# Attention scores of a recommender: 25 groups summed in one PSUM bank by wide products instead of one-column products

## The chip, the cores and the metric

The kernel runs on one core of a Trainium2 chip. Its engines are TensorE (PE, with its weight loads shown as PEld), VectorE (DVE), ScalarE (ACT), GpSimd (POOL) and SyncE (SP); each works through its own list of instructions, and semaphores order them against each other. The metric is the device time of one execution in microseconds, as the median of several runs.

## The reference

There are 50,001 items. For each item two small attentions over its 32 neighbours give two 32-vectors (`a_sus`, `a_inf`). Together with a 64-vector from an embedding table they make a row of 128 numbers per item, for an item in a user's history (`h`) and for a target item (`t`). Then, for 16,384 users with 100 history items each:

```
x      = h * t[:, None, :]                       # 16384 x 100 x 128
z      = relu(einsum("bld,hd->blh", x, W1) + b1) # 128 hidden
scores = einsum("blh,h->bl", z, W2[0])           # one number per user and item
exp_A  = exp(scores) * ((history != target[:, None]) & (history != 0))
attn   = exp_A / (sum(exp_A, -1) ** 0.5)[:, None]
s      = sum(h * attn[..., None])                # one number over all users
pred   = sigmoid(cosine(s * ones, t))            # 16384 results
```

Only the sum of each row of `h` is needed behind the attention, so the kernel keeps that sum in column 0 of its table of rows. Everything is float32.

## The kernel before

The first stage builds the table: POOL gathers 64 neighbour vectors per two tiles of 128 items (`v`, lines 131 to 145), DVE and ACT do the small attentions, and the rows go to two tables in the chip's main memory, `table` (129 numbers: the row's sum and the row) and `ttab` (the target's 128).

The second stage, the user stage, is where the change lies. Users come 128 at a time (`c`, 128 blocks); a block's 100 history items are worked off in 25 groups of `LG` = 4 (`g`). A step `s` is one group of one block, so there are 3,200 steps. In one step

- `gather` (lines 295 to 310): POOL issues four indirect DMAs (L302), each fetching one row of 129 numbers for each of 128 users, into a buffer `h`. There are `HBUF` = 20 such buffers, so POOL may be up to 20 steps ahead;
- `turn` (L318): TensorE transposes the four 128x128 pieces into one PSUM bank `hT_ps` (three such buffers, pool `ps_t`);
- `times_target` (L323, L326): DVE multiplies them by the block's transposed targets `tT` into `xT`, and copies the rows' sums into `hsum`. That copy is the last reader of `h`;
- `hidden` (L335, L337): TensorE multiplies `xT` by `w1T` into `z_ps` (128 hidden x 512 columns), ACT adds the bias and takes the Relu into `z`;
- `scored` (L344): for each of the group's four items TensorE loads `z` of 128 users as the weight and multiplies it by the one column `w2_sb`, which gives one column of the block's `score` tile (128 users x 100 items, one PSUM bank, two buffers in pool `ps_s`).

Once per block `target_rows` (L266) gathers the targets, `target_work` (L278 to L293) transposes them by way of an `hT_ps` buffer and builds the mask `keep`; `weights` (L350) takes the exponential of `score` on ACT into `ea`; `ended` (L355 to L358) multiplies by mask and sums and reduces on DVE.

The order on the engines in this stage is that of the program: a loop over `s` issues the pieces with a skew, `hidden` for step `s - LAG` and `scored` for step `s - 2*LAG` (`LAG` = 3), with `weights` and `ended` hung behind a block's last step:

```python
gather(s); turn(s); times_target(s)
if 0 <= s - LAG < last:      hidden(s - LAG)
if 0 <= s - 2 * LAG < last:  scored(s - 2 * LAG)
done, left = divmod(s - 2 * LAG - NG, NG)
if 0 <= done < UC and left == 0: weights(done)
if 0 <= done < UC and left == 2: ended(done)
```

A short last part (L390 on) combines the sums of all blocks into the results.

Of the kernel before, what the change touches and what calls it, by code (L numbers as in the profile page):

```python
# [10 lines left out]
F32 = mybir.dt.float32  # L11
# [3 lines left out]
AF = mybir.ActivationFunctionType  # L15
# [3 lines left out]
P = 128  # L19
# [5 lines left out]
HID = 128  # L25
B = 16384
L = 100
# [14 lines left out]
UC = B // P  # L42
BSUB = 4
LG = 4
NG = L // LG
W = 1 + D
LAG = 3
# [6 lines left out]
def kernel(  # L54
# [13 lines left out]
    nc = tc.nc  # L68
# [4 lines left out]
    const = ctx.enter_context(tc.tile_pool(name="const", bufs=1))  # L73
# [7 lines left out]
    ident = const.tile([P, P], F32, name="ident")  # L81
# [5 lines left out]
    w2_sb = const.tile([HID, 1], F32, name="w2_sb")  # L87
    nc.sync.dma_start(w2_sb, w2.rearrange("o h -> h o"))
    w1_sb = const.tile([HID, D], F32, name="w1_sb")
    nc.sync.dma_start(w1_sb, w1)  # L90
    w1T = const.tile([D, HID], F32, name="w1T")
    with tc.tile_pool(name="wps", bufs=1, space=bass.MemoryType.PSUM) as wps:
        w1_ps = wps.tile([D, HID], F32, name="w1_ps")
        nc.tensor.transpose(w1_ps, w1_sb, ident)
        nc.vector.tensor_copy(w1T, w1_ps)
# [149 lines left out]
    with (  # L245
# [11 lines left out]
        users, hists = {}, {}  # L257
        rows, got, hT, xT, z = {}, {}, {}, {}, {}

        def history_of(i):  # L260
            hists[i] = u_in.tile([P, BSUB, L], I32, name="hidx")
            nc.sync.dma_start(hists[i], hist_v[i])

        def target_rows(c):
            t = u_t.tile([P, D], F32, name="t")
            nc.gpsimd.indirect_dma_start(  # L266
                out=t,
                out_offset=None,
                in_=ttab[0:ITEMS, :],
                in_offset=bass.IndirectOffsetOnAxis(ap=tidx[:, c : c + 1], axis=0),  # L270
            )
            users[c] = {"t": t, "hidx": hists[c // BSUB][:, c % BSUB, :]}

        def target_work(c):
            u = users[c]
            t = u["t"]
            tT_ps = ps_t.tile([P, LG, P], F32, name="hT_ps")
            nc.tensor.transpose(tT_ps[:, 0, :], t, ident)  # L278
            tT = u_t.tile([D, 1, P], F32, name="tT")
            nc.vector.tensor_copy(tT[:, 0, :], tT_ps[:, 0, :])  # L280
            u["tT"] = tT
            nc.vector.tensor_reduce(tsum[:, c : c + 1], t, AX.X, ALU.add)
            junk = u_t.tile([P, D], F32, name="junk")
            nc.scalar.activation(junk, t, AF.Square, accum_out=tsq[:, c : c + 1])
            keep = u_s.tile([P, L], F32, name="keep")
            idf = u_s.tile([P, L], F32, name="idf")
            nc.vector.tensor_copy(idf, u["hidx"])
            nc.vector.tensor_scalar(keep, idf, 0.0, None, ALU.not_equal)
            nc.vector.scalar_tensor_tensor(
                keep, idf, tidf[:, c : c + 1], keep, ALU.not_equal, ALU.mult  # L290
            )
            u["keep"] = keep
            u["hsum"] = u_s.tile([P, L], F32, name="hsum")  # L293
# [17 lines left out]

        def turn(s):
            c, g = divmod(s, NG)
            if g == 0:
                users[c]["score"] = ps_s.tile([P, L], F32, name="score")
            hT[s] = ps_t.tile([P, LG, P], F32, name="hT_ps")
            for q in range(LG):
                nc.tensor.transpose(hT[s][:, q, :], rows[s][:, q, 1:W], ident)  # L318
# [19 lines left out]

        def scored(s):
            c, g = divmod(s, NG)  # L340
            of = z.pop(s)
            for q in range(LG):
                l = g * LG + q
                nc.tensor.matmul(  # L344
                    users[c]["score"][:, l : l + 1], of[:, q, :], w2_sb, start=True, stop=True
                )

        def weights(c):
            users[c]["ea"] = u_s.tile([P, L], F32, name="ea")
            nc.scalar.activation(users[c]["ea"], users[c]["score"], AF.Exp)  # L350

        def ended(c):
            u = users.pop(c)
# [6 lines left out]
        last = UC * NG  # L360
# [1 line left out]
        history_of(1)  # L362
        target_rows(0)
        target_work(0)
        for s in range(last + 2 * LAG + 4):
            c, g = divmod(s, NG)
            if s < last:
                if g == 0 and c % BSUB == 2 and 0 < c // BSUB and c // BSUB + 1 < UC // BSUB:
                    history_of(c // BSUB + 1)
                if g == 5 and c + 1 < UC:  # L370
                    target_rows(c + 1)
                gather(s)
                turn(s)
                times_target(s)
            if 0 <= s - LAG < last:
                hidden(s - LAG)
            if 0 <= s - 2 * LAG < last:
                scored(s - 2 * LAG)
            if s < last and g == 15 and c + 1 < UC:
                target_work(c + 1)  # L380
            done, left = divmod(s - 2 * LAG - NG, NG)
            if 0 <= done < UC and left == 0:
                weights(done)
            if 0 <= done < UC and left == 2:
                ended(done)

    with (
# [12 lines left out]
        s = f_s.tile([P, 1], F32, name="s")  # L400
# [72 lines left out]
```

## Time and profile before

| | |
|---|---|
| median of 3 runs | 36,520.64 us (36,513.01 to 36,525.43) |
| span of the profiled execution | 36,753.4 us |
| first stage, up to POOL's first gather of the user stage | about 17,531 us |
| user stage | about 19,214 us, 6.0 us a step |
| POOL busy | 25,638.7 us (70%) |
| TensorE busy, matmuls and weight loads | 10,978.4 us (30%) and 8,197.0 us (22%) |
| DVE, ACT busy | 6,839.7 us (19%), 2,598.4 us (7%) |
| granted TensorE clock, whole span and user stage | 0.805 and 0.63 |

The page gives the span of the profiled execution as its only time; it is 232.8 us, or 0.6%, longer than the median of the runs. In the views, "x" is a count of instructions, the number in square brackets is the engine's idle time just before an instruction and what ended it, and "issue" means that the profile shows nothing for which the engine waited. A TensorE instruction's row shows when it was started; the ends of matmuls are modelled.

### The profile page before, as it was taken

The page shows a single profiled execution, that of the slowest core. Times are in us where ns is not written, and L with a number is a line of the kernel's source. Part 1 is how long each engine was busy: PE and PEld are TensorE (multiplying, and loading weights), DVE is VectorE, ACT ScalarE, POOL GpSimd, SP SyncE. Part 2 cuts the span into 40 slices and gives each one's busy share as a digit, 9 for nine tenths or more (in the row PEclk, how much of TensorE's full clock was granted, in tenths as well). Part 3 has the DMA queues.
Part 4 walks back from the last instruction along what each step waited for, and adds up shares of the span by engine and source line. Part 5 has one row for each costly group of instructions (what it writes and reads, how often), then busy time and mean ns, then how long its engine had stood idle before and what let it go on. Part 6 is the DMA issues. An engine that isn't in the chain of part 4 may idle for free. (4 is left out here: it accounts for less than half of the span.)

```text
span 36753.4 us, 140646 instructions
## 1 busy us (share of the span) xinstructions
PE 10978.4 (30%) x44931; PEld 8197.0 (22%) x44931; DVE 6839.7 (19%) x9939; ACT 2598.4 (7%) x5572; POOL 25638.7 (70%) x25446
## 2 busy tenths in 40 slices
PE   0000000000000000000455555555555555555555
PEld 0000000000000000000344444444444444444444
DVE  2222222222222222222111111111111111111111
ACT  0000000000000000000011111111111111111111
POOL 7777777777777777777666666666666666666665
PEclk9999999999999999999766666666666666666666
DMA  1111111111111111111222222222222222222221
GB/s 42 29 27 27 28 27 29 27 27 28 27 29 27 27 28 28 28 27 25 46 45 45 46 45 45 45 46 45 45 45 45 45 46 45 46 45 45 45 45 42
DMA packets 1028095, 1364.65 MB, mean 37 GB/s; under 512 B 559904, under 2 KB 614432, under 8 KB 1027360
## 3 DMA queue, kind: packets, MB, share of 16 engines
q0 software_dynamic: 814080, 1265.42, 16.4%
q10 hardware_dynamic: 151056, 51.51, 0.8%
q1 hardware_dynamic: 62224, 38.72, 0.4%
q8 instruction: 363, 5.95, 0.1%
q14 instruction: 372, 3.05, 0.0%
HBM read 1315.31 MB, written 51.50 MB: 37 GB/s over the span
## 5 line engine op out<-in xcount | busy, mean ns | idle before, releaser
L302 POOL DMA_INDIRECT h<-table,hidx x12800 | 12076.4, 943 | 6922.7 <-issue 3842.1
L140 POOL DMA_INDIRECT v<-in_egeo_dram,nidx x12512 | 13440.9, 1074 | 4062.1 <-issue 3999.8
L344 PEld LDWEIGHTS score<-w_sb,z 128*128 128x128 f32 x25600 | 5127.8, 265 | 7371.6 <-issue 7368.3
L344 PE MATMUL score<-w_sb,z 128*128 128x1 f32 x25600 | 4337.7, 273 | 5275.9 <-issue 5198.2
L278 PE MATMUL hT_ps<-ident,t 128*128 128x128 f32 x128 | 48.6, 380 | 17557.8 <-DMA t<-ttab,tidx 17527.4
L335 PE MATMUL z_ps<-xT,w1T 128*128 128x512 f32 x6400 | 5002.9, 868 | 585.1 <-issue 581.7
L323 DVE TENSOR_TENSOR xT<-hT_ps,tT 128x512 f32<-128x512 f32 x3200 | 2189.8, 688 | 15948.5 <-PE hT_ps L318 7577.8
L278 PEld LDWEIGHTS hT_ps<-ident,t 128*128 128x128 f32 x128 | 35.8, 280 | 17561.6 <-issue 17561.6
L318 PE MATMUL hT_ps<-ident,h 128*128 128x128 f32 x12800 | 3056.8, 360 | 2340.2 <-issue 1889.1
L337 ACT ACTIVATE z<-z_ps,b_sb 128x512 f32<-128x512 f32 x3200 | 2137.4, 686 | 17016.2 <-remote 6414.2
L155 DVE TENSOR_TENSOR prod<-v,own_ps 128x4096 f32<-128x4096 f32 x196 | 864.4, 4410 | 12931.3 <-DMA v<-in_egeo_dram,nidx 12931.3
L318 PEld LDWEIGHTS hT_ps<-ident,h 128*128 128x128 f32 x12800 | 2231.2, 206 | 2730.8 <-issue 2200.1
L335 PEld LDWEIGHTS z_ps<-xT,w1T 128*128 128x128 f32 x6400 | 1440.8, 271 | 876.2 <-issue 875.7
L188 DVE TENSOR_TENSOR wv<-v,ex 128x1024 f32<-128x1024 f32 x782 | 1377.4, 1874 | 315.8 <-ACT ex L172 303.1
L172 ACT ACTIVATE ex<-sc,top 128x32 f32<-128x32 f32 x782 | 227.7, 291 | 16999.8 <-DVE sc L162 10385.7
L162 DVE TENSOR_REDUCE sc<-prod 128x128 f32<-128x4096 f32 x196 | 864.5, 4411 | 6.7
L196 DVE TENSOR_REDUCE att<-wv 128x128 f32<-128x4096 f32 x196 | 864.1, 4409 | 6.0
L326 DVE COPY hsum<-h 128x4 f32<-128x4 f32 x3200 | 537.9, 168 | 0.0
L266 POOL DMA_INDIRECT t<-ttab,tidx x128 | 120.7, 943 | 66.2 <-issue 65.3
L280 DVE COPY tT<-hT_ps 128x128 f32<-128x128 f32 x128 | 37.0, 289 | 593.7 <-remote 343.9
L172 ACT ACTIVATION_READ_ACCUMULATOR ex<-sc,top 128x1 f32 x782 | 146.1, 187 | 0.0
L153 ACT COPY own_ps<-own 128x64 f32<-128x64 f32 x391 | 82.2, 210 | 56.9 <-issue 49.3
(50 smaller groups left out, 638.7 us busy)
## 6 DMA issues: line engine op xcount, KB each, us to landing
h<-table,hidx POOLq DMA_INDIRECT x12800
v<-in_egeo_dram,nidx POOLq DMA_INDIRECT x12512
table<-row ACTq DMA_DIRECT2D x22, 1096.5 KB
own<-in_egeo_dram SPq DMA_DIRECT2D x23, 544.0 KB
row<-in_ehist_dram SPq DMA_DIRECT2D x23, 544.0 KB
ttab<-in_etgt_dram ACTq DMA_DIRECT2D x1, 12500.0 KB
ttab<-row ACTq DMA_DIRECT2D x22, 544.0 KB
hidx<-in_history_dram SPq DMA_DIRECT2D x32, 200.0 KB
```

The lines of the kernel that those rows point to most:

```text
L140: nc.gpsimd.indirect_dma_start(out=v[:, m, k].rearrange("p t d -> p (t d)"), out_offset=None, in_=egeo, in_offset=bass.IndirectOffsetOnAxi ...
L155: nc.vector.tensor_tensor(prod[:, 0:n].rearrange("p m k t d -> p m k (t d)"), v.rearrange("p m k t d -> p m k (t d)"), own_ps[:, 0:n].to_b ...
L162: nc.vector.tensor_reduce(sc[:, 0:n].rearrange("p m t k -> p m k t"), prod[:, 0:n], AX.X, ALU.add)
L188: nc.vector.tensor_tensor(wv[:, m, t].rearrange("p d k -> p k d"), subs[b]["v"][:, m, :, t, :], ex[:, m, t, :].rearrange("p (k o) -> p k o ...
L196: nc.vector.tensor_reduce(att[:, 0:n], wv[:, 0:n], AX.X, ALU.add)
L302: nc.gpsimd.indirect_dma_start(out=rows[s][:, q, :], out_offset=None, in_=table, in_offset=bass.IndirectOffsetOnAxis(ap=users[c]["hidx"][: ...
L318: nc.tensor.transpose(hT[s][:, q, :], rows[s][:, q, 1:W], ident)
L323: nc.vector.tensor_tensor(xT[s], hT.pop(s), users[c]["tT"].to_broadcast([D, LG, P]), ALU.mult)
L326: copy = nc.vector.tensor_copy(users[c]["hsum"][:, g * LG : (g + 1) * LG], rows.pop(s)[:, :, 0:1].rearrange("p q o -> p (q o)"),)
L335: nc.tensor.matmul(z_ps, w1T, xT.pop(s), start=True, stop=True)
L337: nc.scalar.activation(z[s], z_ps, AF.Relu, bias=b1_sb)
L344: nc.tensor.matmul(users[c]["score"][:, l : l + 1], of[:, q, :], w2_sb, start=True, stop=True)
```

## The change

A constant tile `pick` is built at the start: 25 small matrices of 128 x 25, all zeros but for `w2` in column `g` of the `g`-th. For each step `scored` now makes one product, with `pick[:, g, :]` as the weight and the step's whole `z` (512 columns) as the moving operand, into a bank of 25 partitions x 512 columns. The products of a block's 25 steps are accumulated in that bank: step `g` adds the scores of its 4 x 128 items and users to partition `g` and zero to all others. `weights` becomes a copy of the bank to SBUF on ACT. A new piece `exponents`, one step later, turns it back with four TensorE transposes (25x128 to 128x25) into a buffer of `ps_t`, and takes the exponential on ACT into `ea`, in the order that `ea` had before. `ended` moves from two steps behind `weights` to four, and the loop runs two steps longer.

```diff
+    pick = const.tile([HID, NG, NG], F32, name="pick")
+    nc.vector.memset(pick, 0.0)
+    for g in range(NG):
+        nc.vector.tensor_copy(pick[:, g, g : g + 1], w2_sb)
...
         def turn(s):
             c, g = divmod(s, NG)
-            if g == 0:
-                users[c]["score"] = ps_s.tile([P, L], F32, name="score")
             hT[s] = ps_t.tile([P, LG, P], F32, name="hT_ps")
...
         def scored(s):
             c, g = divmod(s, NG)
-            of = z.pop(s)
+            if g == 0:
+                users[c]["bank"] = ps_s.tile([NG, LG, P], F32, name="bank")
+            nc.tensor.matmul(
+                users[c]["bank"], pick[:, g, :], z.pop(s), start=g == 0, stop=g == NG - 1
+            )
+
+        def weights(c):
+            flat = u_t.tile([NG, LG, P], F32, name="flat")
+            nc.scalar.copy(flat, users[c].pop("bank"))
+            users[c]["flat"] = flat
+
+        def exponents(c):
+            flat = users[c].pop("flat")
+            score = ps_t.tile([P, LG, P], F32, name="hT_ps")
             for q in range(LG):
-                l = g * LG + q
-                nc.tensor.matmul(
-                    users[c]["score"][:, l : l + 1], of[:, q, :], w2_sb, start=True, stop=True
-                )
-
-        def weights(c):
+                nc.tensor.transpose(score[:, q, 0:NG], flat[:, q, :], ident[0:NG, 0:NG])
             users[c]["ea"] = u_s.tile([P, L], F32, name="ea")
-            nc.scalar.activation(users[c]["ea"], users[c]["score"], AF.Exp)
+            nc.scalar.activation(
+                users[c]["ea"].rearrange("p (g q) -> p q g", q=LG), score[:, :, 0:NG], AF.Exp
+            )
...
-        for s in range(last + 2 * LAG + 4):
+        for s in range(last + 2 * LAG + 6):
...
             if 0 <= done < UC and left == 0:
                 weights(done)
-            if 0 <= done < UC and left == 2:
+            if 0 <= done < UC and left == 1:
+                exponents(done)
+            if 0 <= done < UC and left == 4:
                 ended(done)
```

## The prediction

> **What bounds the kernel now.** I read the page's totals and costliest groups first, then stretches of the user stage, then single instructions in order of time, then the waits and the end of the chain.
>
> ```profile
> PE 10978.4 (30%) x44931; PEld 8197.0 (22%) x44931; DVE 6839.7 (19%) x9939; ACT 2598.4 (7%) x5572; POOL 25638.7 (70%) x25446
> L302 POOL DMA_INDIRECT h<-table,hidx x12800 | 12076.4, 943 | 6922.7 <-issue 3842.1
> L344 PEld LDWEIGHTS score<-w_sb,z 128*128 128x128 f32 x25600 | 5127.8, 265 | 7371.6 <-issue 7368.3
> L344 PE MATMUL score<-w_sb,z 128*128 128x1 f32 x25600 | 4337.7, 273 | 5275.9 <-issue 5198.2
> L335 PE MATMUL z_ps<-xT,w1T 128*128 128x512 f32 x6400 | 5002.9, 868 | 585.1 <-issue 581.7
> L318 PE MATMUL hT_ps<-ident,h 128*128 128x128 f32 x12800 | 3056.8, 360 | 2340.2 <-issue 1889.1
> L337 ACT ACTIVATE z<-z_ps,b_sb 128x512 f32<-128x512 f32 x3200 | 2137.4, 686 | 17016.2 <-remote 6414.2
> ```
>
> No engine is full. Per group of 128x4 rows (3200 groups) TensorE runs 4 transposes, 2 products of 512 columns (float32 takes two passes) and 8 score products of one column, each with its own weight load: 28 instructions, 16 of them for the scores. Now the stretches (columns: the window's length, then busy time and count of PE, PEld, DVE, ACT, POOL, then the clock, the DMA share, GB/s):
>
> ```profile
> 17531.00:36745.00 19214.00, 10977.44 (x44928) 8196.31 (x44928) 2649.56 (x7553) 2192.09 (x3588) 12197.16 (x12928) 0.63 0.20 45
> 17531.00:17570.00 39.00, 15.43 (x30) 5.84 (x31) 5.21 (x15) 1.78 (x4) 26.41 (x28) 1.00 0.27 67
> 24953.90:24961.00 7.10, 7.10 (x43) 5.52 (x42) 2.16 (x6) 2.06 (x3) 5.57 (x6) 0.88 0.22 50
> 24989.40:25002.20 12.80, 12.80 (x63) 9.78 (x64) 3.09 (x8) 2.53 (x5) 9.70 (x11) 0.72 0.21 48
> 25024.30:25038.20 13.90, 13.90 (x50) 10.80 (x51) 3.88 (x12) 3.11 (x5) 10.55 (x12) 0.50 0.21 48
> 24966.90:24987.20 20.30, 3.92 (x14) 3.01 (x13) 0.77 (x2) 0.69 (x1) 12.69 (x14) 0.56 0.21 47
> 25003.70:25022.00 18.30, 4.16 (x10) 2.25 (x10) 0.00 (x0) 0.00 (x0) 11.74 (x13) 0.59 0.22 49
> 24953.90:24989.40 35.50, 18.34 (x94) 13.82 (x93) 4.39 (x13) 4.17 (x7) 22.64 (x24) 0.69 0.20 45
> ```
>
> POOL's gathers, in order of time:
>
> ```profile
> 24953.91 0.94 POOL L302 DMA_INDIRECT h<-table,hidx  x1 [6.02 <-PE hT_ps L318]
> ...
> 24982.61 0.94 POOL L302 DMA_INDIRECT h<-table,hidx  x1 [0.30 <-issue]
> 24989.45 0.94 POOL L302 DMA_INDIRECT h<-table,hidx  x1 [5.89 <-PE z_ps L335]
> ```
>
> First and last are 24 issues: 28.70/23 = 1.248 us each, 4.99 us a group. 12928 issues would take 16,134 us of the stage's 19,214; the other 3,080 us are POOL standing still for a free `h` buffer. That is the most this change can bring. One cycle is 24 issues (6 groups, 30 us) and a stall of 5.6 us beyond the usual gap: 5.93 us a group.
>
> Why buffers are late (DVE's and TensorE's instructions, in order of time):
>
> ```profile
> 24959.55 0.69 DVE L323 TENSOR_TENSOR xT<-hT_ps,tT 128x512 f32<-128x512 f32 x1 [2.08 <-PE hT_ps L318]
> 24967.44 0.69 DVE L323 TENSOR_TENSOR xT<-hT_ps,tT 128x512 f32<-128x512 f32 x1 [7.09 <-PE z_ps L335]
> 24987.94 0.69 DVE L323 TENSOR_TENSOR xT<-hT_ps,tT 128x512 f32<-128x512 f32 x1 [19.73 <-remote]
> 24962.46 0.63 PE L318 MATMUL hT_ps<-ident,h 128*128 128x128 f32 x4
> 24985.82 1.01 PE L335 MATMUL z_ps<-xT,w1T 128*128 128x512 f32 x1 [1.05 <-issue]
> 24987.22 1.01 PE L335 MATMUL z_ps<-xT,w1T 128*128 128x512 f32 x1 [0.39 <-issue]
> 25005.18 0.16 PE L344 MATMUL score<-w_sb,z 128*128 128x1 f32 x1 [1.26 <-issue]
> 25006.59 0.16 PE L344 MATMUL score<-w_sb,z 128*128 128x1 f32 x1 [1.25 <-issue]
> 25000.17 0.69 DVE L323 TENSOR_TENSOR xT<-hT_ps,tT 128x512 f32<-128x512 f32 x1 [4.53 <-PE hT_ps L318]
> 25022.79 0.69 DVE L323 TENSOR_TENSOR xT<-hT_ps,tT 128x512 f32<-128x512 f32 x1 [21.86 <-PE z_ps L335]
> 17570.35 0.69 DVE L323 TENSOR_TENSOR xT<-hT_ps,tT 128x512 f32<-128x512 f32 x1 [6.39 <-PE hT_ps L318]
> 17587.18 0.69 DVE L323 TENSOR_TENSOR xT<-hT_ps,tT 128x512 f32<-128x512 f32 x1 [16.06 <-PE z_ps L335]
> ```
>
> Transposes drawn as ended at 24963.1 release DVE only at 24987.94, and successive DVE products are 20.5 us apart (22.6 in the next cycle, 16.8 near the stage's start). In that stretch TensorE starts 27 instructions in 20.3 us (20 in 18.3 in the next): 0.75 to 0.92 us each, mean 0.83, waiting for nothing shown. A 512-column product with its load takes 1.40 us there, a one-column product with its load 1.41: the price is per instruction, whatever its size. The windows 2 to 5 of the table run from POOL's start or restart to about the last group that DVE got in time: 61 TensorE instructions in 39 us (the stage's start), then 85, 127 and 101 in 7 to 14 us. So the onset goes by a count rather than by time. The stretch ends 4 us after POOL's last gather. What causes it no row says.
>
> When TensorE is fast (end of the chain, cold clock, then full clock):
>
> ```profile
> 36695.51 1.50 PE score L344 x8
> 36697.00 0.96 PE hT_ps L318 x4
> 36697.96 1.71 PE z_ps L335 x2
> ...
> 36719.90 0.50 PE hT_ps L318 x4
> 36720.39 0.86 PE z_ps L335 x2
> 36721.25 0.79 PE score L344 x8
> ```
>
> A group takes 2.15 to 4.17 us, under POOL's 4.99.
>
> **The change part by part.**
> - *Scores.* 16 instructions a group (8 one-column products, 8 loads of `z`) become 4 (2 passes of 512 columns, 2 loads of a 25-column weight). No row shows a 25-column product; nearest is `z_ps` x2, 0.86 to 1.71 us, against 0.79 to 1.50 for the eight: +0.07 to +0.21 us a fast group, on an engine with slack; bounds from below by half that row (shorter weight). I take +0. In a slow group 12 instructions go: 12 x 0.83 = 10 us of 23.
> - *Turn back, once per user.* Four transposes, 8 instructions per 25 groups: +0.3 a group, so 16.3 instead of 28. In fast stretches 0.5 to 0.96 us a user, 64 to 123 us in all, covered by TensorE's slack.
> - *Copy of the bank on ACT.* Like L337's 686 ns, x128 = 88 us on an engine 7% busy; behind it are queued the next Relus, which have a step of slack. 0, at most 88. Exp now reads a strided 128x100 out of the transposes' bank: 0.
> - *New wait.* TensorE's four transposes wait for that copy, and behind them stand the next step's transposes. The copy follows the previous step's Relu, and between stand a full step of TensorE work (2.15 us or more) against Relu and copy (1.4 us): covered. They also borrow one of three `hT_ps` buffers until Exp. The same loan exists for the target (L278), and its price is a row:
>
> ```profile
> PE hT_ps L318 <- DVE tT L280: 67.6, 17, 7.2
> POOL h L302 <- PE hT_ps L318: 1688.7, 344, 8.7
> ```
>
> 67.6 us in 15,000, so about 90 us a stage; between 0 and that I take +50. The second row is the buffer stall itself.
> - *Setup.* One memset (625 columns, near L323's 0.69 us) and 25 one-column copies on DVE, at most 0.2 us each: 6 us before DVE's first work, which waits for 64 gathers. 0. No DMA is added; the two steps by which `ended` moves back hold buffers with three copies. Tail: one copy and four transposes more, fewer scores: within 2 us.
>
> **The sum.** Before, a cycle: 5 groups in 13.5 fast us (35.5 less the 22 us between DVE's products), slow groups 28 x 0.83 = 23.2 us. With N groups a cycle of T = 4.99 N + 5.6 us: N = 5 + (T - 13.5)/23.2 gives 5.9 and 5.94 us a group; the trace has 5.93. After: of the 5 fast groups some 3 (85/28) lie between restart and onset; 85/16.3 = 5.2 take their place, 7.2 fast groups in 19.5 us; slow groups 16.3 x 0.83 = 13.5 us. N = 7.2 + (T - 19.5)/13.5 gives 9.8, T = 54.5, 5.56 us a group. 0.37 x 3200 = 1,180 us less, +50. The span of 36,753.4 stands 0.6% over the median of 36,520.64, so I take the difference from the median: about **35,400 us**.
>
> [...]
>
> **The rivals.**
> 1. *The slow stretches shrink until POOL alone binds.* For it: TensorE needs 2.15 to 4.17 us of each 4.99. Against it: at the stage's start, before any score was due (they follow six groups behind), 61 instructions already brought the slow stretch on. It gives 36,520 less 3,080, about 60 of which TensorE still needs behind the last gather: 33,500.
> 2. *The onset goes by time or gathers, only the slow price by instructions.* For it: 7.1, 12.8 and 13.9 us lie close together; against it the 39 us. N = 5 + (T - 13.5)/13.5 gives 7.0, 5.79 us a group, 450 less and 50 more: 36,120.
> 3. *Slower.* The slow stretch costs a group its 23.2 us whatever it holds, and the cold 512-column passes lengthen fast groups by 0.21 us: 13.5 us then hold 4.6 groups, N is 5.5, 6.01 us a group, +250, and with the loan and the copy at their bounds (90, 88) 36,950. It decides if instruction count does not matter; the equal spacing of large and small products speaks against it. At worst 0.21 x 3200 + 178 = 850 more, 37,370.
> 4. *The change does nothing: the slow stretch is in the recording alone*, and the timed runs have another bound. Then the time stays near 36,520. Against it: without the stalls the recorded kernel would take 33,700, and the timed runs take 36,520, within 0.6% of the recorded one. [...]
>
> **How the numbers follow.** The sum 0.45; rival 1 0.20; rival 2 0.15; rival 3 0.14; rival 4 0.06. Faster by over 0.2% (about what a measurement of this kernel can tell from no change): 0.80; the same 0.06; slower 0.14. The range takes in the sum and rivals 1 and 2 with their roundings: 33,450 to 36,150. The sum's own range is 34,800 to 35,900.
>
> **What would show it.** The score products fall from 25600 loads to 6400; TensorE's instructions in the stage from 89,856 to about 52,500; POOL's cycle holds some 39 issues instead of 24 between stalls still near 5.6 us; in slow stretches DVE's products come 13 us apart, not 20. It is wrong if those gaps stay at 20 us, if the onset comes after half the instructions, or if TensorE waits for `flat` once a user.

## The result and the profile after

The changed kernel takes 36,157.68 us (median, 36,142.21 to 36,164.7) where the kernel before, run beside it, takes 36,523.04 (36,513.01 to 36,527.8): a ratio of 0.99 with a 95% interval of 0.9886 to 0.9914, 365 us less. Forecast were 35,400 and a range up to 36,150. The sign is right, the gain is a third of the sum's.

The page of the changed kernel (totals, then groups: busy time, mean ns of one, idle time before and what ended it):

```profile
span 36157.2 us, 104181 instructions
...
PE 9955.5 (28%) x26243; PEld 3219.9 (9%) x26243; DVE 6910.6 (19%) x9965; ACT 2692.6 (7%) x5700; POOL 25713.0 (71%) x25446
...
L306 POOL DMA_INDIRECT h<-table,hidx x12800 | 12107.2, 946 | 6300.4 <-issue 3830.4
L144 POOL DMA_INDIRECT v<-in_egeo_dram,nidx x12512 | 13484.1, 1078 | 4013.5 <-issue 3964.1
L325 DVE TENSOR_TENSOR xT<-hT_ps,tT 128x512 f32<-128x512 f32 x3200 | 2198.7, 690 | 15477.9 <-remote 9681.0
...
L337 PE MATMUL z_ps<-xT,w1T 128*128 128x512 f32 x6400 | 4177.9, 741 | 1833.5 <-ACT z L339 1463.2
L320 PE MATMUL hT_ps<-ident,h 128*128 128x128 f32 x12800 | 2520.1, 328 | 5521.0 <-DVE xT L325 3984.9
L345 PE MATMUL bank<-z,pick 128*25 128x512 f32 x6400 | 3978.8, 709 | 0.0
...
L345 PEld LDWEIGHTS bank<-z,pick 128*25 128x25 f32 x6400 | 433.4, 109 | 3095.3 <-issue 3095.3
```

POOL's gathers cost what they did (946 ns, 943 before). POOL's idle time beyond the usual gap fell from 6922.7 - 3842.1 = 3,080 us to 6300.4 - 3830.4 = 2,470: 610 us less. The stage shows the same:

```profile
17531.00:36150.00 18619.00, 9954.09 (x26239) 3219.01 (x26239) 2709.25 (x7551) 2286.34 (x3715) 12227.28 (x12927) 0.72 0.18 47
```

18,619 us instead of 19,214, 595 less; the profiled executions differ by as much, 36,753.4 - 36,157.2 = 596. The medians differ by only 365, because the profiled execution before lay 0.6% over its median and the one after lies on it.

TensorE runs 52,478 instructions in the stage instead of 89,856 (products and weight loads each count as one). Before, its score products had idle time ended by nothing shown (5,198 us of "issue"). Now its transposes wait for DVE (3,985 us of 5,521), because all three `hT_ps` buffers are taken. DVE in turn waits as long as ever, some 12,500 us before and after in the window 20,000 to 35,000 us. The largest of its waits there, first before, then after, and after also some of POOL's and TensorE's (sum in us, times, longest):

```profile
DVE xT L323 <- PE hT_ps L318: 6019.7, 1078, 23.8
...
DVE xT L323 <- remote: 2862.7, 210, 26.0
```

```profile
DVE xT L325 <- remote: 7864.7, 644, 25.1
...
DVE xT L325 <- PE hT_ps L320: 1893.6, 766, 22.4
...
POOL h L306 <- PE hT_ps L320: 1478.7, 478, 9.9
...
PE hT_ps L358 <- ACT flat L351: 548.5, 31, 31.4
```

"Remote" means that a semaphore update stands on record just before the product, but that no instruction which makes such an update is drawn as ending within 1.5 us of it. Here it is TensorE's own semaphore: of the changed kernel's 755 products that start after more than 1 us of idle time ended by "remote", all have an update of it on record, 0.02 us ahead in the median. So the releases themselves come late; TensorE's rows had ended long before. One cycle of the changed kernel, in order of time (rows of TensorE, DVE and POOL):

```profile
24958.19 0.95 POOL L306 DMA_INDIRECT h<-table,hidx  x1 [7.50 <-PE hT_ps L320]
...
24967.06 0.69 DVE L325 TENSOR_TENSOR xT<-hT_ps,tT 128x512 f32<-128x512 f32 x1 [1.65 <-PE hT_ps L320]
...
24971.21 0.66 PE L320 MATMUL hT_ps<-ident,h 128*128 128x128 f32 x4
...
24972.35 0.69 DVE L325 TENSOR_TENSOR xT<-hT_ps,tT 128x512 f32<-128x512 f32 x1 [4.46 <-PE hT_ps L320]
...
24973.62 0.66 PE L320 MATMUL hT_ps<-ident,h 128*128 128x128 f32 x4
...
24984.93 0.69 DVE L325 TENSOR_TENSOR xT<-hT_ps,tT 128x512 f32<-128x512 f32 x1 [11.81 <-remote]
...
25001.96 0.95 POOL L306 DMA_INDIRECT h<-table,hidx  x1 [0.30 <-issue]
25005.93 0.69 DVE L325 TENSOR_TENSOR xT<-hT_ps,tT 128x512 f32<-128x512 f32 x1 [20.23 <-remote]
...
25007.44 0.95 POOL L306 DMA_INDIRECT h<-table,hidx  x1 [4.53 <-issue]
```

Between POOL's restart and 24977 us TensorE transposes seven groups. DVE makes its products in the same order, so the product at 24984.93 belongs to the transposes drawn as ended at 24971.87, 13 us before, and the one at 25005.93 to those ended at 24974.28, 32 us before. POOL issues 36 gathers in this cycle (24 before) and stands still again. The late release is the one that the prediction found; what differs is how far TensorE's starts run ahead of it. Matched in order, group by group, TensorE starts at most 63 instructions between a group's last transpose and the product that waits for it in the kernel before (297 of the 3,200 groups reach it) and from then on its starts go at the pace of the releases, as the 28 between 17587.18 and 17626.38 do. In the changed kernel it starts at most 40 (824 groups reach that): two more groups fill the `hT_ps` buffers, and TensorE stands still.

At the start of the user stage, where POOL has all its buffers free and streams longest, DVE's products before (behind the one at 17587.18, which the prediction shows) and after:

```profile
17626.38 0.69 DVE L323 TENSOR_TENSOR xT<-hT_ps,tT 128x512 f32<-128x512 f32 x1 [38.43 <-remote]
17665.58 0.69 DVE L323 TENSOR_TENSOR xT<-hT_ps,tT 128x512 f32<-128x512 f32 x1 [38.34 <-remote]
```

```profile
17600.27 0.69 DVE L325 TENSOR_TENSOR xT<-hT_ps,tT 128x512 f32<-128x512 f32 x1 [20.85 <-remote]
17622.67 0.69 DVE L325 TENSOR_TENSOR xT<-hT_ps,tT 128x512 f32<-128x512 f32 x1 [21.63 <-remote]
17645.07 0.69 DVE L325 TENSOR_TENSOR xT<-hT_ps,tT 128x512 f32<-128x512 f32 x1 [21.63 <-remote]
17667.47 0.69 DVE L325 TENSOR_TENSOR xT<-hT_ps,tT 128x512 f32<-128x512 f32 x1 [21.63 <-remote]
```

39.20 us for 28 instructions and 22.40 us for 16 are both 1.40 us per instruction. The 16.83 us from 17570.35 to 17587.18 are the same price: between these two releases TensorE's list has 12 instructions and no score yet (four transposes, the two passes of a product, and the six loads). The prediction had priced an instruction at 0.83.

### The profile page after: what moved, and what is told of

Read it like the earlier page. It is cut to its first block, busy times and chain, and to the rows that moved or that the text cites. A ratio compares the mean times of both kernels' runs of the same rounds, so it can differ in the third digit from the quotient of the medians.

```text
span 36157.2 us, 104181 instructions
## 1 busy us (share of the span) xinstructions
PE 9955.5 (28%) x26243; PEld 3219.9 (9%) x26243; DVE 6910.6 (19%) x9965; ACT 2692.6 (7%) x5700; POOL 25713.0 (71%) x25446
## 4 chain that ended last, share of the span: by engine, by line
POOL 37%; another core or an unknown queue 29%; PE 18%; issue 13%; DVE 2%; ACT 1%; DMA 0%; POOLq 0%; SPq 0%; ACTq 0%; DVEq 0%
POOL v L144 37%; PE z_ps L337 7%; PE bank L345 6%; PE hT_ps L320 5%; DVE xT L325 1%; ACT z L339 1%; DVE hsum L328 0%; DMA v<-in_egeo_dram,nidx 0%; PE hT_ps L358 0%; POOL h L306 0%; PE hT_ps L282 0%; ACT flat L351 0%; DVE tT L284 0%; DVE keep L293 0%
## 5 line engine op out<-in xcount | busy, mean ns | idle before, releaser
L306 POOL DMA_INDIRECT h<-table,hidx x12800 | 12107.2, 946 | 6300.4 <-issue 3830.4
L144 POOL DMA_INDIRECT v<-in_egeo_dram,nidx x12512 | 13484.1, 1078 | 4013.5 <-issue 3964.1
L337 PE MATMUL z_ps<-xT,w1T 128*128 128x512 f32 x6400 | 4177.9, 741 | 1833.5 <-ACT z L339 1463.2
L320 PE MATMUL hT_ps<-ident,h 128*128 128x128 f32 x12800 | 2520.1, 328 | 5521.0 <-DVE xT L325 3984.9
L345 PE MATMUL bank<-z,pick 128*25 128x512 f32 x6400 | 3978.8, 709 | 0.0
L320 PEld LDWEIGHTS hT_ps<-ident,h 128*128 128x128 f32 x12800 | 1621.4, 163 | 8660.4 <-DVE xT L325 4994.7
L337 PEld LDWEIGHTS z_ps<-xT,w1T 128*128 128x128 f32 x6400 | 1175.1, 230 | 2056.4 <-ACT z L339 1647.9
L345 PEld LDWEIGHTS bank<-z,pick 128*25 128x25 f32 x6400 | 433.4, 109 | 3095.3 <-issue 3095.3
```

Of the source, the lines that this page charges most:

```text
L144: nc.gpsimd.indirect_dma_start(out=v[:, m, k].rearrange("p t d -> p (t d)"), out_offset=None, in_=egeo, in_offset=bass.IndirectOffsetOnAxi ...
L306: nc.gpsimd.indirect_dma_start(out=rows[s][:, q, :], out_offset=None, in_=table, in_offset=bass.IndirectOffsetOnAxis(ap=users[c]["hidx"][: ...
L337: nc.tensor.matmul(z_ps, w1T, xT.pop(s), start=True, stop=True)
L345: nc.tensor.matmul(users[c]["bank"], pick[:, g, :], z.pop(s), start=g == 0, stop=g == NG - 1)
```

## The experiments

Not every set of runs shows the late release. The kernels of one set ran on the same chip, beside the kernel before. In the sets of `after_again`, `late_turn_c` and `by_three_b`, and in the first measurement, the kernel before takes 36,520 to 36,680 us. In the nine others it takes 31,836 to 31,892 us, and in the kernels traced there all but at most three of DVE's 3,200 products follow their transposes within 3 us. The changed kernel itself was not run in one of the nine; variants of it that keep POOL's pace differ from the kernel before by 0.15% at most there, so the change is worth next to nothing where nothing is late. It isn't the chip alone: `by_three_b` and `one_pass_e` ran on the same one, and the kernel before took 36,531 and 31,892 us there. A set of the second kind can't tell causes of the late release apart, so some kernels were run in several sets, each time under another label (`late_turn` is `e1_late_turn`, `late_turn_b` and `late_turn_c`).

**The change alone, again.** The changed kernel as it is.

> The changed kernel itself, unaltered, beside the old one in the same sitting as the four experiments. In those the old kernel took 31,890 us instead of 36,523, POOL's gathers ran at 1.248 us without a stall and no slow stretch was to be seen. Theory 1 (the change's gain comes only out of the slow stretches): where they are absent the changed kernel takes what the old one takes, 31,880 to 31,930 us, and its profile shows POOL without stalls and no late release of DVE; where they are present it gains about 1% again. Theory 2 (the change does something on a path of its own, the turning back above all): it differs from the old one by more than 100 us even without slow stretches.

36,255.07 us against 36,679.69, a ratio of 0.9887 (0.987 to 0.9903). The gain is the same in another set.

**Is the new wait of the turn-back the lost gain?** The four transposes of line 358 wait for the copy on ACT, and the next groups' transposes stand behind them. In `late_turn` they come four steps later:

```
-        for s in range(last + 2 * LAG + 6):
+        for s in range(last + 2 * LAG + 10):
...
-            if 0 <= done < UC and left == 1:
+            if 0 <= done < UC and left == 5:
                 exponents(done)
-            if 0 <= done < UC and left == 4:
+            if 0 <= done < UC and left == 8:
                 ended(done)
```

> The changed kernel with the turning back four steps later (five steps behind the copy of the bank instead of one) and the block's last sums four steps later too; the same instructions otherwise. Theory 1: the change did shorten the work of the slow stretches, but TensorE then stands still once per 128 users for the copy of the bank, which in a slow stretch comes tens of microseconds late. The waits for it add up to some 550 us with a named releaser and 215 us without, and 138 us for the borrowed buffer, in 15,000 us of the changed kernel: about 1,100 us in the whole stage. Then this kernel takes 35,100 to 35,500 us and that wait is gone from the list. Theory 2 (rival): TensorE waits there for what the slow stretch holds back anyway, and without this wait it waits for DVE instead: 36,050 to 36,200 us.

> The turning back four steps later, once more, beside the old kernel where (and if) the slow stretches are present; of the two chips met so far one has them (old kernel 36,680 us, changed one 36,255) and one has not (31,890). Where they are absent this says nothing new: 31,890 to 31,930 us. Where they are present, theory 1 (the changed kernel loses some 1,100 us of its gain to TensorE's wait for the bank's copy once per 128 users): 35,100 to 35,700 us, and DVE's products around a block's end (groups 4 and 5 and 16 and 17 of the next block) lose their long gaps. Theory 2 (the wait only stands where TensorE would have waited for DVE anyway): 36,150 to 36,300 us, like the changed kernel.

> The turning back four steps later, on whatever chip is given. Three chips have been met: on one the slow stretches are present (old kernel 36,680 us, changed one 36,255), on two they are absent (31,890 and 31,867 us), and there this kernel takes 0.1% more than the old one. Where they are present, theory 1 (the changed kernel loses some 1,100 us of its gain to TensorE's wait for the bank's copy once per 128 users): 35,100 to 35,700 us. Theory 2 (the wait only stands where TensorE would have waited for DVE anyway): 36,150 to 36,300 us.

Without late releases (`e1_late_turn`, and `late_turn_b`, the same kernel again) 31,919.34 and 31,898.48 us, ratios of 1.0009 (1.0 to 1.0019) and 1.001 (1.0 to 1.0019): no difference. `late_turn_c` met late releases: 36,168.2 us, a ratio of 0.9903 (0.9886 to 0.992), no faster than the changed kernel's 0.99. Its waits in the window 20,000 to 35,000 us:

```profile
DVE xT L325 <- remote: 7654.5, 660, 27.0
...
POOL h L306 <- PE hT_ps L320: 1466.0, 496, 8.5
...
PE hT_ps L358 <- DVE xT L325: 166.0, 26, 12.2
...
PE hT_ps L358 <- issue: 26.3, 4, 10.1
```

The wait for `flat` (548.5 us in the changed kernel) is gone, and POOL waits as before. That wait stood in time in which TensorE would have waited anyway.

**Do POOL's short restarts carry it?** The changed kernel has many restarts after which POOL issues only one group's four gathers and stands still again (POOL's and DVE's rows of the changed kernel):

```profile
24579.46 0.95 POOL L306 DMA_INDIRECT h<-table,hidx  x1 [1.40 <-issue]
24580.71 0.94 POOL L306 DMA_INDIRECT h<-table,hidx  x1 [0.30 <-issue]
24581.96 0.95 POOL L306 DMA_INDIRECT h<-table,hidx  x1 [0.30 <-issue]
24583.21 0.94 POOL L306 DMA_INDIRECT h<-table,hidx  x1 [0.30 <-issue]
24592.10 0.94 POOL L306 DMA_INDIRECT h<-table,hidx  x1 [7.95 <-PE hT_ps L320]
```

```profile
24577.95 0.69 DVE L325 TENSOR_TENSOR xT<-hT_ps,tT 128x512 f32<-128x512 f32 x1 [21.63 <-remote]
24590.59 0.69 DVE L325 TENSOR_TENSOR xT<-hT_ps,tT 128x512 f32<-128x512 f32 x1 [11.87 <-remote]
```

One late product frees one buffer just after POOL has stopped; POOL fills it, and the backlog clears only when POOL has stopped a second time, for 7.95 us. `by_three` lets POOL take its gathers three groups at a time, the last group first, so that POOL should wait for three free buffers:

```
-HBUF = 20
+HBUF = 21
...
-                gather(s)
+                if s % 3 == 0:
+                    ahead = [k for k in range(s, s + 3) if k < last]
+                    for k in ahead[-1:] + ahead[:-1]:
+                        gather(k)
```

> The changed kernel with POOL's gathers ordered by three groups (the last of three first) and 21 buffers instead of 20, so that POOL restarts only when three buffers are free; nothing else changed. Where the slow stretches are absent it takes what the changed kernel takes (within 0.1% of the old one). Where they are present, theory 1 (the missing gain lies in POOL's short restarts: 146 of 482 streams of the kernel with the late turn have 16 issues or fewer, because one late group frees one buffer and POOL's four gathers keep the slow stretch up): hardly a stream under 12 issues is left, there are 300 to 350 stalls instead of 480, and the time is 35,500 to 35,900 us (old kernel 36,520 to 36,680). Theory 2 (the total standstill is set by what TensorE has to do in the slow stretches, however it is cut): 36,100 to 36,300 us.

> The changed kernel, but GpSimd takes its gathers three groups at a time and waits, before each three, for the last of the three tiles, so that it never restarts for one free tile alone. In the record of the changed kernel about 469 stalls of mean 5.1 us stand in the user stage, many of them after a stream of only 4 to 16 gathers. Theory A, these short restarts carry the gain that is missing: fewer than 380 stalls, the user stage down by 250 us or more, 35,500 to 35,900 us where the kernel before takes about 36,520. Theory B, the price of a TensorE instruction in the slow stretch carries it, and a short restart is only a stall cut in two: the sum of the stalls stays at 2,200 to 2,500 us, and 36,050 to 36,300 us. Where the chip shows no slow stretch (the kernel before near 31,850 us), both expect no difference and nothing is told apart.

`by_three` met no late release: 31,874.52 us, 1.0012 (1.0002 to 1.0022). `by_three_b` met them: 36,143.62 us, 0.9894 (0.9877 to 0.991), no different from the changed kernel. But the edit did not do what it was for: counted as in the next section, 154 streams of at most 16 gathers stand between two stalls, where the changed kernel has 135. So this run doesn't show what the short restarts cost, and the times fit the second theory without testing the first.

**Does the price go by the count of instructions?** `more_pe` runs ten transposes a group instead of four (28 instructions again), `one_pass` holds `xT`, `z`, `w1T` and `pick` in bfloat16, so that a product takes one pass instead of two (12 instructions; the trace of `one_pass_g` has 14,436 matmuls and 14,530 loads in the window 20,000 to 35,000 us, for some 2,340 groups, with the turning back and the targets among them):

```
-            for q in range(LG):
+            for q in (0, 1, 2, 3, 0, 1, 2, 3, 0, 1):
                 nc.tensor.transpose(hT[s][:, q, :], rows[s][:, q, 1:W], ident)
```

```
-    w1T = const.tile([D, HID], F32, name="w1T")
-    pick = const.tile([HID, NG, NG], F32, name="pick")
+    w1T = const.tile([D, HID], BF16, name="w1T")
+    pick = const.tile([HID, NG, NG], BF16, name="pick")
...
-            xT[s] = u_x.tile([D, LG, P], F32, name="xT")
+            xT[s] = u_x.tile([D, LG, P], BF16, name="xT")
...
-            z[s] = u_z.tile([HID, LG, P], F32, name="z")
+            z[s] = u_z.tile([HID, LG, P], BF16, name="z")
```

> The changed kernel with six of a group's transposes done twice into the same place (10 instead of 4), so that TensorE has 28 instructions per group again, as before the change, all of them small. Theory 1 (the slow stretch has a price per TensorE instruction): the first slow stretch of the user stage, in which DVE's products came 39.2 us apart before and 22.4 us apart after the change (both 1.40 us per instruction), is back at 39 us, and the time is at or above the old kernel's, 36,500 to 37,500 us. Theory 2 (a group has a fixed price in the slow stretch, or the price hangs on one-column products): the products stay 22 us apart and the time within 36,100 to 36,350 us (0.2 to 0.5 us more of fast TensorE work per group, mostly hidden).

> Six of ten transposes per group done twice, so 28 TensorE instructions per group as before the change, once more where the slow stretches may be present. Where they are absent: 31,890 to 31,950 us. Where they are present, theory 1 (1.40 us per TensorE instruction in a long slow stretch): DVE's products in the stage's first slow stretch are 39.2 us apart (28 x 1.40), as in the old kernel, and the time is 36,600 to 37,600 us. Theory 2 (fixed price per group, or a price of one-column products alone): 22.4 us apart, 36,150 to 36,450 us.

> Six of ten transposes per group done twice, so 28 TensorE instructions per group as before the change; on whatever chip is given. On two chips the slow stretches are absent and it took 0.15% more than the old kernel. Where they are present (old kernel 36,520 to 36,680 us, changed one 1% less): theory 1 (a slow stretch has a price per TensorE instruction): DVE's products in the stage's first slow stretch are 39.2 us apart (28 x 1.40), POOL's streams between stalls go back from 36 issues to 24, and the ratio to the old kernel is 1.00 to 1.03. Theory 2 (a fixed price per group, or a price of one-column products alone): 22.4 us apart, streams of 36 issues, ratio 0.99.

> The changed kernel with xT, z, w1T and pick in bfloat16, so that the hidden product and the score product take one pass instead of two: 12 TensorE instructions per group instead of 16 (the results' precision is lower; nothing is left out). Theory 1: DVE's products in the first slow stretch come 12 x 1.40 = 16.8 us apart, and the time falls to 35,000 to 35,800 us even with the turning back where it is. Theory 2 (fixed price per group): 22 us apart, and 36,000 to 36,200 us, since fast TensorE work is not on the path.

> The changed kernel with xT, z, w1T and pick in bfloat16: 12 TensorE instructions per group instead of 16 (lower precision, nothing left out). Where the slow stretches are absent: 31,830 to 31,900 us. Where they are present, theory 1 (price per TensorE instruction): DVE's products in the stage's first slow stretch are 16.8 us apart (12 x 1.40), POOL's streams reach 45 issues or more, and the time is 35,200 to 35,900 us. Theory 2 (fixed price per group): 22.4 us apart and 36,100 to 36,300 us.

> The changed kernel with the tile xT, the tile z, w1T and the 25 weight columns in bfloat16, so that 12 TensorE instructions with their loads are recorded per group where the changed kernel records 16 (the values are coarser; this is for the time alone). Theory B, a price per TensorE instruction in the slow stretch: VectorE's products in a long slow stretch come 12 x 1.40 = 16.8 us apart (22.4 in the changed kernel), the stalls shrink, and the kernel is at 35,300 to 35,900 us where the kernel before takes about 36,520. Theory C, a cost per group that does not go by the count: the products stay 22.4 us apart, and the time stays at 36,050 to 36,250 us. Where the chip shows no slow stretch (the kernel before near 31,850 us), both expect no difference.

> The kernel of one_pass_c once more, since the chip of that run showed no slow stretch. 12 TensorE instructions with their loads per group are recorded where the changed kernel records 16. Theory B, a price per TensorE instruction: VectorE's products in a long slow stretch come 12 x 1.40 = 16.8 us apart (22.4 in the changed kernel), and 35,300 to 35,900 us. Theory C, a cost per group: 22.4 us apart, and 36,050 to 36,250 us. Without slow stretches (the kernel before near 31,850 us) no difference.

> The kernel of one_pass_c and one_pass_d once more, since their chips showed no slow stretch. 12 TensorE instructions with their loads per group are recorded where the changed kernel records 16. Theory B, a price per TensorE instruction: VectorE's products in a long slow stretch come 12 x 1.40 = 16.8 us apart (22.4 in the changed kernel), and 35,300 to 35,900 us. Theory C, a cost per group: 22.4 us apart, and 36,050 to 36,250 us. Without slow stretches (the kernel before near 31,850 us) no difference.

> The kernel of one_pass_c to one_pass_e once more, since their chips showed no slow stretch. 12 TensorE instructions with their loads per group are recorded where the changed kernel records 16 (values in bfloat16, for the time alone). Theory B, a price per TensorE instruction: at the start of the user stage, where the slow stretch is longest, VectorE's products come 12 x 1.40 = 16.8 us apart (22.4 in the changed kernel); a cycle has 9 fast groups where it had 7, and the time is 35,300 to 35,900 us. Theory C, a cost per group: 22.4 us apart there too, and 36,050 to 36,250 us. Without slow stretches (the kernel before near 31,850 us) no difference.

> The kernel of one_pass_c to one_pass_f a last time, since their chips showed no slow stretch. 12 TensorE instructions with their loads per group are recorded where the changed kernel records 16. Theory B, a price per TensorE instruction: at the start of the user stage VectorE's products come 12 x 1.40 = 16.8 us apart (22.4 in the changed kernel); a cycle has 9 fast groups where it had 7, and the time is 35,300 to 35,900 us. Theory C, a cost per group: 22.4 us apart there too, and 36,050 to 36,250 us. Without slow stretches (the kernel before near 31,850 us) no difference.

None of these met late releases. `e2_more_pe`, `more_pe_b` and `more_pe_c`: 31,935.96, 31,911.69 and 31,882.61 us, ratios of 1.0015, 1.0014 and 1.0015 (the last 1.0005 to 1.0024). `e3_one_pass` and, once more each, `one_pass_b` to `one_pass_g`: 31,878.01 us and then 31,824.36 to 31,881.45, ratios of 0.9996 or 0.9997 (0.9987 to 1.0006). So where releases are in time, neither 12 nor 28 instructions a group matter by more than 0.15%, and what a count between is worth where they are late stays untried; the two kernels' own rows (39.20, 22.40 and 16.83 us) are all there is on it.

**What binds where nothing is late?** First the window of the user stage in `late_turn_b`, then POOL's rows of its page, then DVE's products in order of time:

```profile
15640.00:31870.00 16230.00, 11850.80 (x26242) 3176.20 (x26242) 2750.85 (x7573) 2346.14 (x3726) 12199.11 (x12928) 0.81 0.21 54
```

```profile
L306 POOL DMA_INDIRECT h<-table,hidx x12800 | 12078.4, 944 | 3901.5 <-issue 3194.0
L144 POOL DMA_INDIRECT v<-in_egeo_dram,nidx x12512 | 11804.4, 943 | 3829.7 <-issue 3751.9
```

```profile
20019.24 0.69 DVE L325 TENSOR_TENSOR xT<-hT_ps,tT 128x512 f32<-128x512 f32 x1 [4.42 <-PE hT_ps L320]
20024.07 0.69 DVE L325 TENSOR_TENSOR xT<-hT_ps,tT 128x512 f32<-128x512 f32 x1 [3.99 <-PE hT_ps L320]
20029.08 0.69 DVE L325 TENSOR_TENSOR xT<-hT_ps,tT 128x512 f32<-128x512 f32 x1 [4.24 <-PE hT_ps L320]
```

POOL's idle time of 3901.5 us is 12,800 gaps of 0.30 us and 62 us more: POOL hardly ever stands still, and DVE's products follow each other as POOL's groups do, about 5.0 us apart. `e4_pool_pace` adds a small POOL instruction behind each gather; `sp_rows` fetches the rows of `h` by plain DMAs of SP, consecutive rows instead of those that the history names:

```
+        idle = u_t.tile([P, D // 2], F32, name="idle")
...
+                nc.gpsimd.memset(idle, 0.0)
```

```
-                got[s].append(
-                    nc.gpsimd.indirect_dma_start(
-                        out=rows[s][:, q, :],
...
+                at = (s * LG + q) % 390 * P
+                got[s].append(nc.sync.dma_start(rows[s][:, q, :], table[at : at + P, :]))
```

> The changed kernel with a small memset of a scratch tile on POOL behind each gather of the user stage, so that POOL issues more slowly than every 1.25 us. It asks whether the slow stretch needs POOL at its full pace. If it does, the slow stretches get rarer or shorter and TensorE keeps up: the stage becomes 12,928 issues at the new period, with hardly a stall, and may be shorter than the 18,619 us of the changed kernel if the period stays under 1.44 us. If it does not, the stalls stay as they are (some 5 us each) and the time grows by about 12,900 times the memset's share, less what falls into the stalls: 36,500 to 38,500 us.

> The changed kernel with the rows of the user stage fetched by SP with plain DMAs (128 neighbouring rows of the table each, the same bytes) instead of POOL's indirect ones; it leaves out the lookup by history, so its results are not the reference's. It asks what the slow stretch needs, where it is present. Theory 1 (POOL's own gathers keep the other engines' semaphores back): no slow stretch is left, DVE's products follow TensorE's transposes within 1 us throughout, and the stage is bound by SP's DMAs or by TensorE's 2.2 to 4.4 us a group, 7,000 to 14,000 us. Theory 2 (the traffic of the rows as such, or TensorE's own instructions): DVE's products still come up to 20 us late.

`e4_pool_pace` takes 32,403.93 us, 1.0161 (1.0145 to 1.0178) of the kernel before: 514 us more, 0.04 us for each of 12,800 gathers. `sp_rows`, in its single run, takes 23,483.95 us. Its user stage:

```profile
15600.00:23490.00 7890.00, 7802.78 (x26242) 2668.01 (x26242) 2746.40 (x7586) 2348.73 (x3735) 149.21 (x159) 1.00 0.43 110
```

Without POOL's gathers the stage takes 7,890 us, and TensorE is busy in 7,803 of them: 2.44 us a group. Where nothing is late, POOL's issue of gathers is the bound: 16,230 us, twice what TensorE needs here. Whether the late release needs POOL's gathers was not seen, since this set had none.

**What differs between the two kinds of sets?** `by_three` and `by_three_b` are one kernel, with late releases in the second alone. In the views of their DMAs (issues, and the median us until a transfer is recorded as landed), first `by_three`, then `by_three_b`:

```profile
h<-table,hidx POOLq DMA_INDIRECT x12800, 2.5
v<-in_egeo_dram,nidx POOLq DMA_INDIRECT x12512, 2.4
```

```profile
h<-table,hidx POOLq DMA_INDIRECT x12800
v<-in_egeo_dram,nidx POOLq DMA_INDIRECT x12512
```

The second has no landing times, since most of its semaphore records are missing. Counted over the traces, `by_three` has 438,553 records of semaphore updates, 409,464 of them by DMAs (16 for each of 25,440 gathers, and some more), and `by_three_b` 79,566 and 58,820. All other kernels fall into the same two kinds: 430,000 to 456,000 records without late releases, 80,000 to 91,000 with them (the kernels before and after in the record among these). The updates themselves took place in both, since each gather's readers wait for it. In the table stage of `by_three_b` some 2,840 are recorded in each 2,000 us, one every 0.70 us in the mean, in bunches; in `by_three` 26,170. In the changed kernel's slow stretch from 17,590 to 17,660 us it is 100 records in 70 us, again one every 0.70, though the gathers there come every 1.25 us; in the shorter one from 24,972 to 25,002 us it is 57 in 30 us. Twice 0.70 us is the price of a TensorE instruction in the longest slow stretches, and also the distance of the table stage's gathers in such a set (last section). What holds the releases back, what loses the records, and whether the two have one cause, no run shows.

## Why the prediction was wrong, point by point

**What bound the kernel** was read rightly: POOL's gathers and, beyond them, POOL standing still for `h` buffers that are released late. The runs without late releases show what rival 1 supposed, a stage of 16,230 us in which POOL alone binds (the forecast's floor was 16,134). But there the kernel before has nothing to lose either.

**The onset** came out as forecast. Counted from about 18,500 us to shortly before the stage's end, over the cycles with a stream of 28 us or more (467 before, 332 after), the median count of groups that DVE gets in time is 5 before and 7 after (forecast: 5 and 7.2). From POOL's restart to the last of them TensorE starts 28 instructions and as many loads before, 33 and as many after, in 7.3 us and 12.0 us. So the count stays near its value and the time does not, and rival 2, whose 36,120 us is nearest the result, is not what happened. With the loads the counts are 56 and 66. The lead that TensorE's starts reach and never pass is 63 in the kernel before and 40 in the changed one, so there the 66 is not such a lead, and why it comes out so near the 56 stays open. That the 7.2 was met is partly luck: it rests on the 85 instructions of one cycle, and 56 in their place would have given 6.4 (three of the five fast groups left, and 56/16.3 = 3.4).

**The failed step is the price of a slow group**, "16.3 x 0.83 = 13.5". The 0.83 was read from cycles in which a stream of 24 gathers ended the slow stretch after some 20 us, and carried over to cycles of 36 gathers. It isn't one number, and the gap that it was read in was cut short: the one that ends at 24987.94 ends 4.4 us behind POOL's last gather, with the stream, before 28 instructions had shown their full price. In those cycles the first gap of more than 6.5 us between two DVE products has a mean of 12.8 us before and 10.1 after, the second 17.2 and 17.0. All 375 second gaps before end behind the stream's last gather, by 4.5 us in the median, so their 17.2 is a lower bound of the price; after the change 170 of 328 end within the stream, with a mean of 16.4. Per instruction that is 0.46 and at least 0.61 before, 0.62 and 1.04 after, and 1.40 in the longest stretches of both kernels. Fewer instructions let POOL stream longer, and later in a stream each one costs more. The prediction's own sign of error, gaps that stay at 20 us, is there: 21.0 us in the cycle shown. Put into the prediction's form, N = 7.2 + (T - 19.5)/22.4 with T = 4.99 N + 5.6 gives N = 8.5 (34 gathers); with 17.0 in place of 22.4, 9.0 (36). Counted were 34.1 gathers and a stall of 5.72 us (24.4 and 5.74 before, forecast 39 and 5.6; the usual gap of 0.30 is in the 5.72 and 5.74), over streams of 17 or more: 333 of them, 483 before. A group costs 5.89 us before and 5.63 after in these, 0.26 x 3200 = 830 us less where 1,180 were forecast.

**A term was missing**: the short restarts. Streams of at most 16 gathers rose from 72 to 135, with stalls of 3.4 and 3.6 us: 490 - 240 = 250 us given back (over the whole stage 79 and 148 of them). That they are a cost and not a part of a stall that would come anyway is argued from the count, not shown, since `by_three` did not remove them.

**The small terms** held: nothing shows a cost of the 512-column passes (709 ns each, 109 for a load), and the turn-back's wait costs nothing that can be measured, as `late_turn_c` showed. The +50 for the borrowed buffer was not measured by itself; the sum closes without it. The wait held for another reason than the one given: TensorE does wait for `flat`, 31 times in the 15,000 us of the window (some 103 blocks of users), which the prediction had as covered and named as a sign of error; but it waits there in time in which it would have waited anyway. So 830 - 250 = 580 us, against 595 in the trace.

**The base** took the rest. The sum was made against the profiled execution and carried over whole to the median. Of the 596 us between the profiled executions 231 are that 0.6% of the first one, and don't exist between the medians. Together: 35,400 + 350 (price) + 250 (restarts) - 50 + 231 is 36,181, and 36,158 was measured.

**Rival 3** (slower) had half the truth: the first slow group of a cycle costs nearly the same with fewer instructions (10.6 and 10.0 us, over the gaps that end within the stream), but in the longest stretches the cost falls with their count (39.20 to 22.40 us), and more groups pass before the first slow one. The equal second gaps (17.2 and 17.0) don't speak for it, since those before are cut short. **Rival 4** had the wrong consequence: the timed runs agree with the profiled one (36,158 and 36,157) and moved with the change. Of its cause, the recording, the traces show only that missing records and late releases come together (some 80,000 to 91,000 records with late releases, 430,000 to 456,000 without); whether one brings the other no run shows, since no kernel here could leave the recording out. The prediction gave rival 4 a chance of 0.06, and it argued only from the times. Why some sets have the late releases stays open too. The four sets with them hold neither `more_pe` nor `one_pass`, the nine without them hold one of these; whether that is more than chance wasn't tried.

## What to carry to other kernels

Look first whether a trace is complete: a view of the DMAs without landing times said here, before any experiment, that most semaphore records were missing, and in the sets where they are there the wait that the change was to shorten does not exist. Read a price from a stretch that isn't cut short and is as long as the one it is to be used in (the same instruction cost 0.46 to 1.40 us, and the change itself lengthened the stretch), and count cycles, their length and their short forms, because here a saving at the consumer that stalls its producer went partly into longer cycles (24 gathers before, 34 after) that cost more per instruction. Match each product with the instructions that it waits for, in order: the rows of TensorE ran up to 63 instructions ahead of their releases, and only the match showed how late these were. Make the sum for the execution that was profiled and say how much of it lies in that execution alone: at 0.6% above the median it took 231 us of a gain of 596.

## What the runs showed that was not expected

- The same kernel takes 36,520 to 36,680 us in some sets of runs and 31,836 to 31,892 in others, and in the first most semaphore records are missing from the trace, one being kept every 0.70 us (mean of the table stage and of the longest slow stretch).
- TensorE's work can be drawn as done 13 to 32 us before those who wait for it go on (the cycle shown; up to 82 us before and 65 after at the start of the stage), while POOL streams indirect DMAs. The backlog clears at once, 3.0 us (25002.91 to 25005.93, after) or 4.4 us (24983.55 to 24987.94, before) behind the end of POOL's last gather.
- The table stage pays as well: a gather of line 144 takes 1,078 ns in the mean after the change and 943 in `late_turn_b`. Its rows in the changed kernel's trace, 1.40 us apart, twice the mean distance of 0.70 us between the records there:

```profile
10000.73 1.09 POOL L144 DMA_INDIRECT v<-in_egeo_dram,nidx  x1 [0.30 <-issue]
10002.13 1.09 POOL L144 DMA_INDIRECT v<-in_egeo_dram,nidx  x1 [0.30 <-issue]
```

- Plain DMAs of SP filled the same buffers with as many rows in less than half of the time that POOL needs to issue the gathers (7,890 us for the whole stage, 16,230 with gathers).
